# A two-layer bi-WKV and mixture-of-experts kernel: shared tiles at other steps, one exponential per unit of layer 1, and a fixed order in layer 1's input stage

## The chip, the cores and the metric

The kernel runs on one core of one Trainium2 chip, in fp32 throughout. The metric is the device time of one launch in microseconds (us), here the median of three runs. A core has five engines that run side by side, each through its own list of instructions in order: PE (TensorE: matmuls and transposes), DVE (VectorE), ACT (ScalarE: activations and copies), POOL (GpSimd: indirect gathers and scatters) and SP (SyncE, which here only issues transfers). They wait for each other through semaphores. ACT has to load a table (1.28 us in this trace) when it changes between families of functions, here between exponential and logarithm, sigmoid, and SiLU.

## The reference, cut to what matters

`x` is (4, 512, 512): 4 batches of 512 tokens with 512 channels, 2048 tokens in all. Two layers each add their result to `x`:

```python
def bi_wkv(r, k, v, w, u, time_emb):          # called with r = x, k = v = fside
    tf = sigmoid(sum(time_emb))               # one number per batch
    decay = exp(-exp(w)) * (0.5 + 0.5 * tf)   # per channel and batch
    ek = exp(min(k, 30)); ekv = ek * v
    nf, df = forward scans over tokens of ekv and ek:  a = a * decay + ekv_t
    nb, db = the same scans backward
    euk = exp(min(u + k, 30))
    num = nf + nb - ekv + euk * v
    den = df + db - ek + euk
    return sigmoid(r) * (num / max(den, 1e-8)) * (0.8 + 0.2 * tf)

x = x + ffn0(bi_wkv(x, fside, fside, w0, u0, cond))
x = x + ffn1(bi_wkv(x, fside, fside, w1, u1, cond))
```

`ffn0` normalises its rows (RMS norm with a weight), sends each token to the 2 best of 8 experts (`silu(h Wg) * (h Wu)` with 256 inner channels, then `Wd`), and adds a shared expert of the same form for all tokens. `ffn1` sends each token to the 6 best of 32 experts (352 inner channels, at most 512 tokens an expert) and adds a shared expert with 704 inner channels.

## The kernel before

**Tiles and units.** P is 128. The tokens are 16 tiles of 128 (NT); the channels are 4 blocks of 128 (NC). Layer 0's scans work on 16 units (b, c): one batch and one block of channels, 128 channels on the partitions by 512 tokens. `kA` holds k turned, `zT` the output of bi-WKV turned (channels on the partitions), `acc` rows of x or gathered rows. PSUM, the memory that matmuls write to, [...] given out by name: "tr" (turned tiles) 2, "den" 2, "num" 1, "g" 2, "pl" 1 in layer 0.

**Layer 0's steps.** The loop at L657 has a step for each unit and one more. Step n holds `sums(n-1)` (PE adds the forward and backward terms of num and den of the unit before), `front(n+1)`, `front_exps(n+1)` (two exponentials on ACT), `mid(n)` (the scans, on DVE), `back(n-1)` (the quotient: ACT makes `r`, the reciprocal, out of den with three activations at L448 to L450, DVE multiplies), `turn(n+3)` (k's transposes), and, at certain steps, the routing of a batch (`route_*`, `write_slots`, with POOL's writes of a table), `row_turn` and `row_out` (z turned back to rows for the gathers) and `logits0`. On the four compute engines the order is the order of the code (a manual schedule).

**Shared tiles of layer 0.** The shared expert runs tile by tile: `share_up` (PE, 16 matmuls at L594), `share_silu` (ACT), `share_hid` (DVE), `share_turn` (PE transposes at L612, ACT copy at L614), `share_down` (PE, four matmuls at L622), `share_put` (ACT copy, and SP writes the rows to `xb`). `pairs0` places tiles at steps: the up in the step that is its key, the hidden product one step later, turn, down and put two steps later. Tiles 0 to 5 are placed so; `early` is the first tile after them. Tiles 6 to 12 run in the tail after the loop (L722 to L764), with the down of a tile one turn of the loop behind its own transposes. Tiles 13 to 15 (from LATE) run after the routed experts (L979 to L990), where a down follows its own turn.

**Exponentials for layer 1.** Layer 1's scans need exp of k plus a bias twice per unit (`ek` and `euk`). `exps1_upto` (L643, L644) writes both into tiles that are free: 10 units by the end of the tail, and 6 units inside the routed stage, where `wkv1_rest` puts twelve exponentials and two table loads (L956 to L958) on ACT between the first and the second token tile of expert 1.

**Routed experts.** `routed` (L769) goes through experts and token tiles of 128 slots: POOL gathers rows, PE turns them (`pza`), ACT copies them out with a scale (`zgT`, L814), PE multiplies (`pgate` L862, `pup` L866), ACT and DVE make the hidden rows, PE turns them (`phT`), multiplies down (`pout`, L838), and POOL scatters and adds to `xa` or `xb`. DVE runs layer 1's scans (`wkv1`) beside it. In the text (1,2) is token tile 2 of expert 1.

**Layer 1's input stage (L993 to L1035).** For each token tile: DVE adds the summands (L1015, L1017), PE turns the result (`pt`, L1020), ACT takes the sigmoid (`sx`, L1022), DVE multiplies with `kA` into `zT` (L1023), PE makes 32 logits (`plg`, L1025) and turns `zT` back (`pz`, L1030), ACT copies the rows (`zr`, L1032), and SP writes them to `z1d`. Tiles 13 to 15 come first. Here the order on SP is fixed, and that of the other engines is left to the framework's scheduler. After it come layer 1's shared expert with its routing (L1107 to L1119) and its routed experts.

Of the kernel before, what the change touches and what calls it, by code (L numbers as in the profile page):

```python
# [18 lines left out]
P = 128  # L19
# [12 lines left out]
def adaln_ffn_kernel(  # L32
# [88 lines left out]
    banks.update(pool=ps, tr=2, den=2, num=1, g=2, pl=1)  # L121
# [97 lines left out]
    for l in range(2):  # L219
# [18 lines left out]
        decay.append((dec, cap, lom, inv))  # L238
    neg_min = const.tile([P, 1], F32, name="neg_min")
# [34 lines left out]
    def scans(l, b, c, v):  # L274
# [6 lines left out]
        nc.vector.tensor_scalar(v[:, :, 0], v[:, :, 0], inv, None, ALU.mult)  # L281
        for h in range(2):
            nc.vector.tensor_tensor_scan(v[:, h, :], dec.to_broadcast([P, S]), v[:, h, :], 0.0, ALU.mult, ALU.add)
# [146 lines left out]
    def mid(n):  # L430
# [6 lines left out]
        scans(0, b, c, v)  # L437
# [194 lines left out]
    rows, cols = [acc[:, t, :] for t in range(NT // 2)], [zcols(n) for n in range(NU)]  # L632
    spare = rows[:2] + cols[:4] + rows[2:] + cols[4:12]
    e1 = {}
    done = 0

    def exps1_upto(m):
        nonlocal done
        while done < m:
            b, c = units[done]  # L640
            kT = kA[:, c, b * S : (b + 1) * S]
            ek, euk = e1[done] = spare[2 * done], spare[2 * done + 1]
            nc.scalar.activation(ek, kT, AF.Exp, bias=decay[1][2][:, c, b : b + 1])  # L643
            nc.scalar.activation(euk, kT, AF.Exp, bias=uch[1][:, c : c + 1])  # L644
            done += 1


    pairs0 = {7: (0, 1), 10: (2, 3), 13: (4, 5)}
    early = 6
# [7 lines left out]
    for n in range(NU + 1):  # L657
# [36 lines left out]
        for t in pairs0.get(n, ()):  # L694
            share_silu(t)
        if c == 3 and b + 1 < NB or n == 0:
            sigmoids(b + 1 if n else 0)
        if n in pairs0 or c == 3 and b + 1 < NB or n == 0:
            nc.scalar.preload_act_table_set(EXP_LN)
        if n < NU:  # L700
            mid(n)
# [4 lines left out]
        if c == 2 and b >= 1:  # L706
            route_max(b - 1)
        if c == 3 and b >= 1:
            route_top(b - 1)
            route_pay(b - 1)  # L710
        if n == NU:
            share_up(early)
# [4 lines left out]
        if n >= 12:  # L717
            exps1_upto(n - 11)
# [3 lines left out]
    pz = [row_turn(t, "den" if t % 2 else "tr") for t in range(NT - TB, NT)]  # L722
    logits0(NB - 1)
    route_v(NB - 1)
# [5 lines left out]
    row_out(*pz[3])  # L730
    share_up(early + 1)
    share_silu(early)
    share_silu(early + 1)
# [14 lines left out]
    share_hid(early + 1)  # L748
    share_turn(early)
    for t in range(early + 2, LATE):  # L750
        share_up(t)
        share_silu(t)
        share_turn(t - 1)
        share_down(t - 2, "den")
        share_hid(t)
        share_put(t - 2)
        if t == 10:
            exps1_upto(8)
    share_turn(LATE - 1)
    for t in (LATE - 2, LATE - 1):  # L760
        share_down(t, "den")
        share_put(t)
    exps1_upto(10)
    nc.scalar.preload_act_table_set("silu_and_others")  # L764
    order.close()
# [165 lines left out]

    late_out = [zT[:, h, :S] for h in range(NT - LATE)]
    with tc.tile_pool(name="r0", bufs=1) as rp, tc.tile_pool(name="px0", bufs=1, space=PSUM) as px:
        third[0] = rp.tile([P, W0], F32, name="third0")
        for n in range(10, NU):
            spare += [rp.tile([P, S], F32, name=f"spare{n}_{h}") for h in range(2)]


        def wkv1(n):
            b, c = units[n]  # L940
            kT = kA[:, c, b * S : (b + 1) * S]
            ek, euk = e1[n]
            v = rp.tile([P, 2, S], F32, tag="v2", name=f"v2_{n}", bufs=1)
            cap = decay[1][1][:, c, b : b + 1]
            nc.vector.tensor_scalar(v[:, 0, :], ek, cap, None, ALU.min)
            nc.vector.tensor_tensor(v[:, 1, :], v[:, 0, :], kT, ALU.mult)
            scans(1, b, c, v)
            d, s = v[:, 0, :], v[:, 1, :]
            nc.vector.scalar_tensor_tensor(d, euk, E30, d, ALU.min, ALU.add)
            nc.vector.scalar_tensor_tensor(euk, euk, E30, kT, ALU.min, ALU.mult)  # L950
# [210 lines left out]
```

## Time and profile before

| | |
|---|---|
| time, three runs | 1561.48, 1562.08, 1569.90 us; median 1562.08 |
| the profiled execution | 1565.78 us; its span in the trace is 1563.8 us |
| busy over the span | PE 1424.2 us (91%), DVE 678.2 (43%), POOL 564.6 (36%), ACT 415.2 (27%) |
| instructions | 16280 |
| moved by transfers | 184.98 MB |

The profile comes from one execution. Every row of its timeline has a start, a length, the engine, the line of the code, the tiles written and read, and, in square brackets, how long the engine had been idle before and what ended that. The granted clock is the clock of PE as a share of full speed; it is either full or half at a moment, so that 0.78 over a stretch means that nearly half of it ran at half clock. PE's idle time is the time to look for wherever PE is the bound; in the first stage it is DVE's.

The stages by their times: layer 0's steps up to some 208 us, its tail to 258.8, the routed experts of layer 0 to 519, the three late shared tiles to 545, layer 1's input stage to 592.5, and the rest of layer 1 to the end.

### The profile page before, as it was taken

The numbers are of one execution on the slowest core, as the hardware profiler recorded it, in microseconds if no ns is written. First come the engines' busy times: TensorE is split into PE (matmuls) and PEld (weight loads), VectorE is DVE, ScalarE is ACT, GpSimd is POOL, SyncE is SP. The second block draws the span as 40 slices with busy tenths as digits, with TensorE's granted clock in tenths as the row PEclk, the third lists the DMA queues.
The fourth block names the chain that finished last, engine by engine and source line by source line (L and its number), as shares of the span: only waits on it lengthen the run. The fifth ranks groups of instructions, "written<-read, shape, count | busy, mean of one in ns | idle before, by whom it ended". The sixth has DMA issues, their size and how long they took to land. (4 is left out here: it accounts for less than half of the span.)

```text
span 1563.8 us, 16280 instructions
## 1 busy us (share of the span) xinstructions
PE 1424.2 (91%) x5033; PEld 849.2 (54%) x5033; DVE 678.2 (43%) x1189; ACT 415.2 (27%) x984; POOL 564.6 (36%) x563
## 2 busy tenths in 40 slices
PE   5778888989788788999999999999999999999997
PEld 3344456757566584444444555655655555555554
DVE  7999844999991145431111222222222222222221
ACT  6657626564344341000001111111111111111110
POOL 1020232756655100056662333344434343343332
PEclk9889889989998888999999999999999999999999
DMA  9301115544545560001115554656636485555442
GB/s 340 128 14 41 41 39 170 89 100 74 132 96 135 180 233 37 1 1 56 48 56 168 138 152 113 172 165 175 170 86 161 123 271 118 147 163 147 113 97 43
DMA packets 117932, 184.98 MB, mean 118 GB/s; under 512 B 19480, under 2 KB 64556, under 8 KB 117784
## 3 DMA queue, kind: packets, MB, share of 16 engines
q1 hardware_dynamic: 81912, 125.54, 23.5%
q0 software_dynamic: 35296, 56.63, 19.5%
q8 instruction: 67, 1.10, 0.3%
q10 hardware_dynamic: 576, 1.05, 0.2%
q14 instruction: 81, 0.66, 0.1%
HBM read 151.28 MB, written 52.64 MB: 130 GB/s over the span
## 5 line engine op out<-in xcount | busy, mean ns | idle before, releaser
L862 PE MATMUL pgate<-w,zgT 128*128 128x352 f32 (+1 forms) x656 | 198.3, 448 | 19.9 <-ACTq L920 9.3
L838 PE MATMUL pout<-w,hT 128*128 128x512 f32 (+1 forms) x432 | 201.2, 598 | 4.9 <-ACT hT L829 4.1
L866 PE MATMUL pup<-w,zgT 128*128 128x352 f32 (+1 forms) x656 | 192.1, 437 | 0.0
L843 POOL DMA_INDIRECT out_dram<-ob,put x52 | 82.9, 1595 | 281.6 <-DVE ob L842 147.7
L797 POOL DMA_INDIRECT acc<-z1d,put x119 | 123.2, 1035 | 134.6 <-PE pza L810 65.4
L862 PEld LDWEIGHTS pgate<-w,zgT 128*128 128x128 f32 x656 | 126.1, 200 | 76.1 <-issue 17.5
L365 POOL DMA_INDIRECT table<-pay,r1sloti x96 | 93.3, 972 | 191.3 <-DVE hid L1110 164.6
L878 DVE SCALAR_TENSOR_TENSOR hrow<-pup,tab,sgt 128x352 f32<-128x352 f32 x84 | 49.1, 584 | 255.1 <-issue 131.2
L866 PEld LDWEIGHTS pup<-w,zgT 128*128 128x128 f32 x656 | 125.5, 195 | 49.9
L842 DVE COPY ob<-pout 128x512 f32<-128x512 f32 x84 | 58.1, 692 | 174.4 <-PE pout L838 167.2
L838 PEld LDWEIGHTS pout<-w,hT 128*128 128x128 f32 (+1 forms) x432 | 76.8, 192 | 71.7 <-issue 54.1
L365 POOL DMA_INDIRECT table<-r0pay,r0sloti x32 | 34.1, 1064 | 184.6 <-DVE r0sloti L355 167.0
L833 ACT COPY hT<-phT 96x128 f32<-96x128 f32 x84 | 21.9, 261 | 287.0 <-DVE hT L831 287.0
L810 PEld LDWEIGHTS pza<-ident,acc 128*128 128x128 f32 x584 | 71.8, 141 | 44.9 <-issue 27.5
L820 ACT COPY zgT<-pza 128x256 f32<-128x256 f32 x103 | 38.3, 372 | 209.7 <-DVE zgT L819 158.0
L1107 PE MATMUL g<-zT,w 128*128 128x512 f32 (+1 forms) x192 | 88.1, 602 | 3.6 <-DVE lg L1039 3.6
L810 PE MATMUL pza<-ident,acc 128*128 128x128 f32 x584 | 86.5, 273 | 5.1 <-DMA acc<-z0d,put 2.5
L838 PE MATMUL pout<-zT,hT 128*128 128x512 f32 (+1 forms) x192 | 87.8, 593 | 0.0
L1107 PE MATMUL u<-zT,w 128*128 128x512 f32 (+1 forms) x192 | 86.3, 592 | 0.0
L1116 PE MATMUL o<-w,hid 128*128 128x512 f32 (+1 forms) x192 | 83.8, 592 | 0.0
L797 POOL DMA_INDIRECT acc<-z0d,put x51 | 62.5, 1225 | 58.5 <-issue 17.0
L862 PE MATMUL pgate<-zT,zgT 128*128 128x352 f32 x256 | 81.0, 459 | 0.0
(268 smaller groups left out, 2070.4 us busy)
## 6 DMA issues: line engine op xcount, KB each, us to landing
w<-in_L_ffn_w_dram SPq DMA_DIRECT2D x44, 704.0 KB, 4.6
zT<-in_L_ffn_w_dram SPq DMA_DIRECT2D x20, 704.0 KB, 5.9
w<-in_L_ffn_w_dram SPq DMA_DIRECT2D x22, 512.0 KB, 8.5
zT<-in_L_ffn_w_dram SPq DMA_DIRECT2D x10, 512.0 KB, 4.5
w<-in_L_ffn_w_dram SPq DMA_DIRECT2D x22, 192.0 KB, 8.5
acc<-in_x_dram SPq DMA_DIRECT2D x4, 1024.0 KB
xa<-acc SPq DMA_DIRECT2D x4, 1024.0 KB, 11.2
z0d<-zr SPq DMA_DIRECT2D x16, 256.0 KB, 2.0
```

Source lines behind the costliest of these rows:

```text
L365: ins = nc.gpsimd.indirect_dma_start(out=table, out_offset=bass.IndirectOffsetOnAxis(ap=sloti[:, t, j : j + 1], axis=0), in_=pay[:, t, j, ...
L797: nc.gpsimd.indirect_dma_start(out=rows(e, s), out_offset=None, in_=zd, in_offset=bass.IndirectOffsetOnAxis(ap=put_at[:, e * NS + s : e * ...
L810: nc.tensor.transpose(pza[which][:, c * P : (c + 1) * P], rows(e, s)[:, c * P : (c + 1) * P], ident)
L820: nc.scalar.copy(dst[:, h:, :], pza[which][:, h * P :].rearrange("p (c t) -> p c t", c=h))
L838: nc.tensor.matmul(po, hT[:m, j, :], dv[:m, j, :], start=(j == 0), stop=(j == nf - 1))
L842: nc.vector.tensor_copy(row, po)
L843: nc.gpsimd.indirect_dma_start(out=outs[n % len(outs)], out_offset=bass.IndirectOffsetOnAxis(ap=at, axis=0), in_=row, in_offset=None, boun ...
L862: nc.tensor.matmul(pg, zt[:, c, :], gv[:, c, :], start=(c == 0), stop=(c == NC - 1))
L866: nc.tensor.matmul(pu, zt[:, c, :], uv[:, c, :], start=(c == 0), stop=(c == NC - 1))
L878: nc.vector.scalar_tensor_tensor(hrow, pu, tab[:, col, 1:2], sgt, ALU.mult, ALU.mult)
L1107: nc.tensor.matmul(p[:m], wv[:, c, f : f + m], zT[:, c, cols], start=(c == 0), stop=(c == NC - 1))
L1116: nc.tensor.matmul(po, hid[:m, j, i * P : (i + 1) * P], dv[:m, j, :], start=(j == 0), stop=(j == len(FCH) - 1))
```

## The change

In layer 0 the shared tiles go to steps 6, 10, 14 and 15 (seven tiles instead of six), their SiLU comes after the step's other ACT work, and in the tail each down follows directly on its own turn. The PSUM banks go from two to one for "den" and from two to three for "g".

For layer 1 one exponential per unit is made instead of two. The second comes from it on DVE, by a factor per channel and batch (`ratio`, made once at the start). All sixteen are made in the steps from 8 on and in the tail, and `wkv1_rest` is gone. Two units of `wkv1` run in the tail, cut into steps by `yield`.

In layer 1's input stage the order on ACT, PE and DVE is written out: the turn of the next tile, then logits and rows of this one, then the product of the next. Tile 12 joins tiles 13 to 15 at the head, with loads of its own.

```diff
-    banks.update(pool=ps, tr=2, den=2, num=1, g=2, pl=1)
+    banks.update(pool=ps, tr=2, den=1, num=1, g=3, pl=1)
...
+    ratio = const.tile([P, NC, B], F32, name="ratio")
+    nc.vector.tensor_tensor(ratio, uch[1].unsqueeze(2).to_broadcast([P, NC, B]), decay[1][2], ALU.subtract)
+    nc.scalar.activation(ratio, ratio, AF.Exp)
...
-            ek, euk = e1[done] = spare[2 * done], spare[2 * done + 1]
-            nc.scalar.activation(ek, kT, AF.Exp, bias=decay[1][2][:, c, b : b + 1])
-            nc.scalar.activation(euk, kT, AF.Exp, bias=uch[1][:, c : c + 1])
+            nc.scalar.activation(e1[done], kA[:, c, b * S : (b + 1) * S], AF.Exp, bias=decay[1][2][:, c, b : b + 1])
             done += 1
...
+    def wkv1(n, pool, bufs):
+        b, c = units[n]
+        kT, e = kA[:, c, b * S : (b + 1) * S], e1[n]
+        v = pool.tile([P, 2, S], F32, tag="v2", name=f"v2b_{n}", bufs=bufs)
+        d, s = v[:, 0, :], v[:, 1, :]
+        nc.vector.tensor_scalar(d, e, decay[1][1][:, c, b : b + 1], None, ALU.min)
+        nc.vector.tensor_tensor(s, d, kT, ALU.mult)
+        nc.vector.tensor_scalar(e, e, ratio[:, c, b : b + 1], E30, ALU.mult, ALU.min)
+        yield
+        yield from scans(1, b, c, v)
...
-    pairs0 = {7: (0, 1), 10: (2, 3), 13: (4, 5)}
-    early = 6
+    pairs0 = {6: (0, 1), 10: (2, 3), 14: (4, 5), 15: (6,)}
+    early = 7
...
-        for t in pairs0.get(n, ()):
-            share_silu(t)
...
+        exps1_upto(max(0, n - 7) if n < 12 else min(2 * n - 18, 12))
+        for t in pairs0.get(n, ()):
+            share_silu(t)
+        if n in pairs0:
+            nc.scalar.preload_act_table_set(EXP_LN)
...
+    share_turn(early - 1)
     share_up(early + 1)
+    exps1_upto(NU)
     share_silu(early)
-    share_silu(early + 1)
+    share_down(early - 1, "den")
...
+    scans1 = (step for n in range(ahead1) for step in wkv1(n, wk, 3))
+    for t in range(early + 1, LATE):
+        if t > early + 1:
+            share_up(t)
         share_silu(t)
         share_turn(t - 1)
-        share_down(t - 2, "den")
+        share_down(t - 1, "den" if t % 2 else "num")
         share_hid(t)
-        share_put(t - 2)
-        if t == 10:
-            exps1_upto(8)
+        share_put(t - 1)
+        next(scans1, None)
+        next(scans1, None)
     share_turn(LATE - 1)
-    for t in (LATE - 2, LATE - 1):
-        share_down(t, "den")
-        share_put(t)
-    exps1_upto(10)
+    share_down(LATE - 1, "den")
     nc.scalar.preload_act_table_set("silu_and_others")
+    share_put(LATE - 1)
+    through(scans1)
...
-        def wkv1_rest():
-            exps1_upto(NU)
-            nc.scalar.preload_act_table_set("silu_and_others")
-            for n in range(10, NU):
-                wkv1(n)
...
-            for n in range(10):
-                wkv1(n)
+            for n in range(ahead1, NU):
+                through(wkv1(n, rp, 2))
...
-                {1: wkv1_rest, E0 - 2: shared_again, E0 - 1: lambda: scale_weights(*shared0[:2])},
+                {E0 - 2: shared_again, E0 - 1: lambda: scale_weights(*shared0[:2])},
...
+    first = [*range(LATE, NT), LATE - 1]
...
+    with tc.manual_schedule(
+        engines={mybir.EngineType.Activation, mybir.EngineType.PE, mybir.EngineType.DVE}
+    ):
+        turns = first + list(range(LATE - 1))
+        add(turns[0])
+        add(turns[1])
+        product(turns[0], gate(turns[0]))
+        for i, t in enumerate(turns):
+            if i + 2 < NT:
+                add(turns[i + 2])
+            if i + 1 < NT:
+                sx = gate(turns[i + 1])
+            rows_out(t)
+            if i + 1 < NT:
+                product(turns[i + 1], sx)
```

`gate(t)` is `pt` and the sigmoid `sx`, `product(t, sx)` the product into `zT`, and `rows_out(t)` is `plg`, `pz`, the copy `zr` and the write to `z1d`: the same operations as before, cut into functions.

## The prediction

> **What bounds the kernel now.** I read the rows of slices first, then the stages that the change touches, then single rows. Columns in the first fence are 40 slices of 39.1 us in tenths; in the second start:end, length, busy us (instructions) of PE, PEld, DVE, ACT, POOL, granted clock, DMA share, GB/s.
>
> ```profile
> PE   5778888989788788999999999999999999999997
> DVE  7999844999991145431111222222222222222221
> PEclk9889889989998888999999999999999999999999
> ```
> ```profile
> 0.00:258.80 258.80, 195.90 (x681) 112.56 (x682) 191.04 (x443) 151.28 (x277) 45.27 (x61) 0.92 0.30 106
> 258.80:519.00 260.20, 226.14 (x933) 165.35 (x934) 211.12 (x208) 123.20 (x366) 149.70 (x116) 0.93 0.49 109
> 519.00:545.00 26.00, 22.06 (x72) 14.40 (x71) 4.73 (x8) 4.38 (x11) 1.58 (x1) 0.90 0.61 190
> 545.00:592.50 47.50, 37.30 (x256) 34.38 (x256) 19.89 (x33) 19.81 (x34) 0.00 (x0) 0.78 0.68 241
> 592.50:1563.80 971.30, 942.80 (x3092) 522.53 (x3092) 251.44 (x501) 116.52 (x298) 368.07 (x385) 1.00 0.44 116
> ```
> These are layer 0's steps and tail, its routed experts, the three late shared tiles, layer 1's input stage, and the rest of layer 1. PE is the bound of the last 971 us, which no edit touches. In the first stage DVE is the bound until about 208:
> ```profile
> 100.00:120.00 20.00, 14.22 (x45) 6.32 (x46) 19.20 (x36) 10.49 (x25) 9.15 (x8) 0.91 0.09 29
> ...
> 208.80:258.80 50.00, 42.03 (x161) 27.96 (x161) 11.12 (x58) 27.09 (x52) 17.31 (x19) 0.96 0.33 109
> ```
> and PE in the tail. The lowest clock, 0.78, stands in the stage whose order is fixed by the change.
>
> **The change part by part.** All sums are against the profiled execution, 1565.78 us with a span of 1563.8; it stood 3.7 above the median, 1562.08, and I carry the difference over to the median.
>
> *One constant at the start.* `ratio` is a small DVE operation (neighbours there take 0.18) and a small Exp (0.20) between the ACT work of `lom` at 13.08 and the copy of `kA` at 13.20, with hand-overs: +0.6, between 0 (the first sums wait for k's load as well) and +0.7.
>
> *Shared tiles moved to other steps.* Steps run at 19.2 of 20 us on DVE, so PE work moved between them (3.5 us an up, 1.9 a down) is hidden by DVE and worth nothing either way. The one step where DVE waits is 14:
> ```profile
> 179.21 0.16 DVE L519 TENSOR_TENSOR v<-v,rsg 128x4 f32<-128x4 f32 x1 [4.71 <-ACT rsg L512]
> ```
> ACT came late because it stood behind the SiLU of tiles 4 and 5, whose sums PE ended at 173.6. With these two a step later and the SiLU behind the exponentials, 4.7 us of DVE go. But tiles 4 and 5's turn and down (3.7) and the up of tile 7 (3.5) then stand on PE ahead of the last row turns: row turns end near 207.8 instead of 208.85. So 1 of the 4.7 arrives.
>
> In the tail one up less remains (tiles 8 to 12 instead of 7 to 12), but `share_down` now follows its own turn, and waits for the copy between. The late tiles already run so:
> ```profile
> 538.48 1.98 PE L622 MATMUL pout<-third,shT 128*128 128x512 f32 x4 [0.61 <-ACT shT L614]
> ```
> They repeat each 6.26 us (531.23 to 537.49 at L612) where the tail has 5.39 (225.18 to 230.57). Four exponentials (0.62 each) and a table load (1.28) stand on ACT ahead of tile 7's SiLU, so I put the up of tile 9 near 223.8, where before that of tile 8 starts at 220.03. Four periods of 6.26 and a last turn and down of 2.7 end at 251.5; before, the last down ends at 252.5: −1 (−4 if the loop keeps 5.39, +3 if the exponentials reach PE in full).
>
> Two DVE units of layer 1 (13.2 us each) go into the tail beside 11 us of DVE work in 50: hidden by PE, ending near 253.
>
> *Exponentials and table loads between the tail and routed tile (0,0).* Two table loads and the exponentials that filled ACT from 253.18 to 258.33 go. That looks like −5. But the first `zgT` copy, at 258.34, also waits for the last shared row written by SP:
> ```profile
> 253.19 0.32 SPq L629 DMA_DIRECT2D xb<-so_rows  x1
> ...
> 258.40 0.37 SPq L142 DMA_DIRECT2D third<-in_L_ffn_w_gate_dram  x1
> ```
> SP's own next load of `third` waits for the same write and goes at 258.40, so that write took 5.1 us, in a queue with 512 KB of weights on either side. The order on SP is kept. So 0, as long as the write keeps its 5.1 us. The gathers and POOL's table writes have some 7 us to spare and stay covered.
>
> *Exponentials in routed tiles.* These are on the path. PE's first gates of (1,0) and (1,2), then the same of expert 2, which has no exponentials beside it:
> ```profile
> 326.20 1.97 PE L862 MATMUL pgate<-w,zgT 128*128 128x256 f32 x8 [1.25 <-PEq L920]
> ...
> 347.86 1.91 PE L862 MATMUL pgate<-w,zgT 128*128 128x256 f32 x4
> 386.31 1.53 PE L862 MATMUL pgate<-third,zgT 128*128 128x256 f32 x6 [2.15 <-PEq L920]
> ...
> 401.83 1.46 PE L862 MATMUL pgate<-third,zgT 128*128 128x256 f32 x6
> ```
> 21.66 against 15.52: 6.1, and 1.16 for the gate at 347.86, which runs at half clock after the stall (3.05 where a warm one takes 1.89): −7.1. ACT was blocked for 10 us (333.44 to 343.50), but expert 2 shows waits on its gather and on POOL that would appear in expert 1 too, so I don't take the 10. DVE's scans, now with one exponential multiplied up to two on DVE (still about 13.2 a unit), end after 14 units near 441 instead of 477, and are first needed at 545: 0.
>
> *Layer 1's input stage.* Per tile: four transposes (`pt`), a sigmoid, a product, eight small logit matmuls (`plg`), four transposes (`pz`). Before, a scheduler ran `pt` of several tiles ahead and left `pz` for the end; now each tile is `pt` of the next, `plg`, `pz`. At full clock a tile takes some 1.9 us (0.47 + 0.81 + 0.47 and hand-overs), at half clock 0.88 + 1.57 + 0.89 = 3.34. So all turns on the clock:
> ```profile
> 548.50:561.50 13.00, 13.00 (x63) 12.81 (x64) 4.74 (x8) 3.55 (x7) 0.00 (x0) 0.50 1.03 366
> 561.50:562.00 0.50, 0.50 (x5) 0.27 (x4) 0.20 (x1) 0.27 (x1) 0.00 (x0) 0.68 0.93 341
> 562.00:582.00 20.00, 18.87 (x166) 17.72 (x166) 12.02 (x19) 9.97 (x19) 0.00 (x0) 1.00 0.34 118
> ```
> PE's records are unbroken from 548.5 to 561.5 and the clock stayed at 0.50. All clock changes of this trace lie on a grid of 3.413 us, so I worked out for each grid window how much of it streamed columns (128 columns at half clock: 0.213 us). Of windows at half clock, the 19 that went up had at least 0.797, the 13 that stayed at most 0.735; of windows at full clock, the 19 that dropped had at most 0.345 and the lowest that stayed had 0.391. The four here had 0.609, 0.588, 0.505 and 0.797; the last held twelve transposes in a row.
>
> [...] by the rows its share is (512 + 256 + 512 columns = 2.134 us) / 3.34 = 0.64, under 0.735, and it never comes up again. [...]
>
> Does it fall at all? After `pt` of the first two tiles (ended at 546.55 on the old time line) PE now waits for the table load (546.40, 1.28), sigmoid (0.60) and product (0.69), to 549.2: 2.65 us of 3.413 empty, against a wait of 1.66 at 548.34 before, which was enough to fall. It holds only if the grid cuts the gap in halves with work on both sides.
>
> Cold: 549.2 + 16 × (1.57 + 0.89) + 14 × 0.88 = 600.9; the clock falls only at the end of the gap's window, so some work after the gap still runs at full clock (−0.9); from the end of the last `pz` (588.96) to the first matmul of the shared stage (592.56) stand 3.6 more. 603.6 against 592.56: +11 (+7 if windows with runs of `pz` and `pt` back to back bring the clock up half-way, +13 if hand-overs show as gaps). Warm: 549.2 + 16 × 1.9 + 3.6 = 583.2: −9.4. The loads, 8.4 MB from 534 at 366 to 390 GB/s, are in by 556 and bound neither, so tile 12's own pair of loads and the earlier pool cost nothing; `z1d` writes are now 3.3 us apart, so that three `zr` buffers suffice.
>
> Sum: +0.6 − 1 + 0 − 7.1 + 11 = +3.5: 1569.3 against the profiled 1565.78, or 1565.6 against the median.
>
> **The rivals.** *The input stage stays warm.* For it: windows with a share of 0.391 stayed at full clock, and a warm mix streams about half of its time (1.07 of 1.9 us), so once warm it stays warm. Against it: the gap of 2.65 us at its head. It gives 3.5 − 11 − 9.4 = −16.9: 1545.2.
>
> *Slower: one bank for `den`.* Sums of unit n now can't start before the ACT reads of unit n−1's `den` are over. Between these DVE has about 9.1 us of cover (the rest of `back` 2.1, `front` 0.9, `mid` 6.1) for 1.8 to 3.4 of sums, 2.05 of Relu, Ln and Exp, and queueing on both engines. If queueing passes 4, each late step costs the rest; 1.5 us at 10 of 16 steps is +15: 1581. Against it: PE is busy 14 of 20 us there, so queues are short.
>
> *The exponentials' gain isn't there:* expert 1 keeps 21.66 because the gather or POOL is late instead. That is +7.1: 1572.7.
>
> **How the numbers follow.** The forecast has 0.65, warm 0.20, the bank 0.08, no gain 0.07. The forecast's own bounds are the start (0 to 0.7), the tail (−4 to +3), the routed gain (−10 to −5) and the cold stage (+7 to +13): 1557 to 1573. About 0.5% (7.8 us) is what a measurement of this kernel can tell from no change. Of the 0.65, 0.50 lies within it and 0.15 above; warm is faster (0.20); the bank and most of the lost gain (0.05) are slower, the rest within: slower 0.28, same 0.52. The range leaves out most of the bank: 1543 to 1576.
>
> **What would show it.** Right: DVE's wait of 4.71 at step 14 gone; the first `zgT` copy still about 5 us behind the last shared row's issue; expert 1's first to third gate near 15.5; in the input stage a granted clock near 0.5 over some 50 us, with `pt` rows at 0.88 a tile. Wrong: that stage at clock 1.0 within 36 us; or DVE waits on `r` at each step.

## The result and the profile after

The changed kernel takes 1576.03 us (median of six runs, 1574.61 to 1578.09), the kernel before beside it 1566.47 us (six runs, 1561.48 to 1572.99): a ratio of 1.0062, 95% interval 1.0035 to 1.0089. It is slower by 0.6%, 9.6 us, where +3.5 us (0.2%) was forecast, and just above the upper end of the range, 1576. Part of the distance to the forecast time of 1565.6 is its base: the 1562.08 of the first three runs was low, the median of six is 4.4 us higher, and in the three later comparisons before's median was 1569.53, 1572.09 and 1569.87. The profiled execution has a span of 1572.8 us against 1563.8.

The page's slices of the changed kernel (columns as before):

```profile
PE   4878877989788799999999999999999999999997
DVE  7999858999950235431111222222222222222221
PEclk9899999999998958999999999999999999999999
```
In the row of the clock the fifteenth slice, 550 to 590 us, is 5 where before it was 8: layer 1's input stage, 541 to 598. The same stages as before, cut at the same instructions:

```profile
0.00:262.60 262.60, 194.84 (x681) 112.13 (x681) 215.46 (x472) 148.57 (x275) 46.87 (x61) 0.92 0.30 104
262.60:514.80 252.20, 220.06 (x932) 160.96 (x932) 187.70 (x196) 112.85 (x350) 147.57 (x116) 0.95 0.50 110
514.80:541.00 26.20, 21.07 (x73) 13.83 (x73) 4.04 (x7) 5.95 (x14) 1.58 (x1) 0.93 0.68 211
541.00:598.10 57.10, 51.27 (x256) 50.46 (x256) 20.81 (x34) 20.00 (x33) 0.00 (x0) 0.54 0.56 201
598.10:1572.80 974.70, 945.71 (x3092) 524.13 (x3092) 251.57 (x500) 116.61 (x298) 368.16 (x385) 0.99 0.44 116
```
The input stage is 57.1 us instead of 47.5, at a clock of 0.54 instead of 0.78, with PE busy for 51 of 57. Cut more finely, by the starts of matmuls on PE, one profile against one profile:

| from, to | before | after | change | forecast |
|---|---|---|---|---|
| start, last logits of layer 0 (`pl`) | 208.81 | 208.54 | −0.27 | } −0.4 together |
| to the last down of the tail (last `so` matmul) | 43.09 | 47.40 | +4.31 | } |
| to the first gate of the routed experts | 6.91 | 6.72 | −0.19 | 0 |
| routed experts and late tiles, to the first `pt` | 286.78 | 278.32 | −8.46 | −7.1 |
| input stage, to the shared stage's first matmul | 46.97 | 57.14 | +10.17 | +11 |
| to the last matmul | 961.33 | 964.99 | +3.66 | 0 |

The terms for the transition, the routed experts and the input stage hold within 1.4 us here. Two don't: the tail, and the part behind the edit. The other profiles on record show how firm each row is. The start took 205.3 to 208.8 us in six profiles with before's steps (the one in the table is the slowest; mean 206.6), and 207.8 to 209.8 in twelve with the changed ones (mean 208.9), so that the steps lost some 2.3 us rather than won 0.3. The tail took 41.9 to 43.1 us in before's order and 46.8 to 49.1 in seven profiles with the changed one. The routed experts took 286.1 to 288.6 us in five profiles with before's exponentials and 272.6 to 284.3 (mean 277.9) in eleven with the changed ones. The lines of the changed kernel are numbered some 20 higher behind the edit: L862 is L885, L838 is L861, L622 is L626.

**Steps and tail.** Windows of a step and of the tail:

```profile
100.00:120.00 20.00, 18.11 (x63) 8.39 (x62) 19.34 (x34) 13.20 (x27) 9.39 (x8) 0.94 0.15 53
208.50:262.60 54.10, 40.19 (x146) 24.83 (x144) 35.44 (x85) 19.06 (x43) 14.73 (x15) 0.91 0.30 99
```
DVE still bounds the steps, though PE has four more busy microseconds in this one. Its wait of 4.71 at step 14 is gone; the waits over 1 us that it has in the steps are 1.85 at 73.25 and 2.59 at 197.12, where PE's `pos` is late (before had a wait of 3.84 on it too, at 202.52, which the prediction passed over). After the steps it waits longer than before: 8.87 us at 211.57 for ACT's squares, where before has 3.30 at 210.49. The end of the steps came near the time put down (the row turns end at 208.6 us; 207.8 was forecast, and 0.6 for the constant), but the gain against before is luck: before's profile was its slowest of six up to there, and on the average nothing is left of the 4.7 us of DVE.

In the tail before shows turn and down back to back, each 5.39 us after the last:

```profile
225.18 0.38 PE L612 MATMUL sph<-ident,shr 128*128 128x128 f32 x2
225.40 1.88 PE L622 MATMUL so<-w,shT 128*128 128x512 f32 x4
...
230.57 0.38 PE L612 MATMUL sph<-ident,shr 128*128 128x128 f32 x2
```
In the changed kernel PE shows:

```profile
224.47 3.75 PE L626 MATMUL so<-w,shT 128*128 128x512 f32 x4 [3.04 <-DVE counts L765]
228.02 3.94 PE L598 MATMUL sg<-w,zT 128*128 128x256 f32 x16
231.80 0.38 PE L616 MATMUL sph<-ident,shr 128*128 128x128 f32 x2
232.78 1.98 PE L626 MATMUL so<-w,shT 128*128 128x512 f32 x4 [0.61 <-ACT ssg L603]
```
The period of 6.26 us with its wait of 0.61 is there as forecast, but it starts at 228.02 instead of 223.8. The first row says why: tile 7's down waits 3.04 us for DVE's copy of the expert counts (`counts`), which reads the "num" bank that this down wants. The down then runs at half clock, 3.75 us for 1.98. The clock had fallen before that wait: the window that ends at 221.84 streams 0.19 of its time, as PE has only small matmuls there and waits 1.54 us for tile 7's hidden row. The second profile of the changed kernel has the same wait, 3.02 us.

**Between the tail and the first gate:**

```profile
257.23 0.32 SPq L633 DMA_DIRECT2D xb<-so_rows  x1
...
262.23 0.37 SPq L142 DMA_DIRECT2D third<-in_L_ffn_w_gate_dram  x1
```
```profile
262.07 1.14 ACT L837 ACTIVATE zgT<-pza,chan 128x128 f32<-128x128 f32 x4 [4.87 <-DMA xb<-so_rows]
```
ACT is free now, and `zgT` still comes 4.84 us after the last shared row is issued (5.15 before). Nothing was gained by removing the exponentials there.

**The routed experts:** first and third gate of expert 1, the same of expert 2.

```profile
328.37 1.99 PE L885 MATMUL pgate<-w,zgT 128*128 128x256 f32 x8 [0.81 <-ACTq L943]
...
346.38 2.76 PE L885 MATMUL pgate<-w,zgT 128*128 128x256 f32 x8
...
383.21 1.99 PE L885 MATMUL pgate<-third,zgT 128*128 128x256 f32 x8 [0.81 <-ACTq L943]
```
18.01 us from the first to the second row, where 21.66 was before and 15.5 forecast. The rest of the gain lies on either side: to expert 2's first gate it is 6.95 us from the routed stage's start (127.50 to 120.55), for a forecast of 7.1. The whole stage is 8.46 us shorter in this pair of profiles and about 9 on the average of those on record, with a spread of 12 us in the changed order.

**The input stage:**

```profile
544.38 1.08 PE L1031 MATMUL plg<-gateT,zT 128*128 128x32 f32 x8 [2.30 <-DVE zT L1025]
...
549.78 1.75 PE L1031 MATMUL plg<-gateT,zT 128*128 128x32 f32 x8
551.34 1.09 PE L1036 MATMUL pz<-ident,zT 128*128 128x128 f32 x4
552.23 1.06 PE L1018 MATMUL pt<-ident,acc 128*128 128x128 f32 x4
...
598.12 6.67 PE L1129 MATMUL g<-zT,w 128*128 128x512 f32 x8 [3.55 <-DVE lg L1061]
```
The gap at the head (2.30 us; forecast 2.65), then the regular turn of `plg`, `pz`, `pt`, 3.31 us a tile (forecast 3.34), without a gap in PE's records. Thirteen grid windows in a row stream 0.625 to 0.656 of their time (forecast 0.64), and all thirteen stay at half clock. The last row is the head of the shared stage: its first eight matmuls need 6.67 us instead of before's 5.37. PE's clock is at half there up to 604.13, for 6.01 us of them; in before it is so up to 595.95, for 3.39 us.

**The rest of layer 1.** Of the +3.66 us behind the edit, 1.3 are this head. Two waits before `phT` matmuls grow by some 0.4 us each. The rest is one window at half clock (1266.32 to 1269.73), far behind the edit, at a gate of one of layer 1's experts:

```profile
1266.97 3.90 PE L885 MATMUL pgate<-w,zgT 128*128 128x352 f32 x8
```
Before's row at the same place ran at full clock:

```profile
1259.04 2.53 PE L862 MATMUL pgate<-w,zgT 128*128 128x352 f32 x8
```
In the changed kernel PE had waited 2.24 us just before it, in before 1.83. The second profile of the changed kernel has a wait of 2.17 us at this place and no half clock behind it.

### The profile page after: what moved, and what is told of

It is laid out like the page before. It is cut to its first block, busy times and chain, and to the rows that moved or that the text cites. A ratio compares the mean times of both kernels' runs of the same rounds, so it can differ in the third digit from the quotient of the medians.

```text
span 1572.8 us, 16267 instructions
## 1 busy us (share of the span) xinstructions
PE 1433.0 (91%) x5033; PEld 861.5 (55%) x5033; DVE 679.6 (43%) x1206; ACT 404.0 (26%) x967; POOL 564.2 (36%) x563
## 5 line engine op out<-in xcount | busy, mean ns | idle before, releaser
L885 PE MATMUL pgate<-w,zgT 128*128 128x352 f32 (+1 forms) x656 | 197.5, 446 | 17.8 <-PEq L943 7.0
L861 PE MATMUL pout<-w,hT 128*128 128x512 f32 (+1 forms) x432 | 200.1, 595 | 1.4 <-DVE hT L854 0.8
L885 PEld LDWEIGHTS pgate<-w,zgT 128*128 128x128 f32 x656 | 125.2, 198 | 73.9 <-issue 26.0
L901 DVE SCALAR_TENSOR_TENSOR hrow<-pup,tab,sgt 128x352 f32<-128x352 f32 x84 | 49.1, 584 | 255.9 <-issue 131.2
L861 PEld LDWEIGHTS pout<-w,hT 128*128 128x128 f32 (+1 forms) x432 | 76.4, 191 | 67.4 <-issue 53.5
L861 PE MATMUL pout<-zT,hT 128*128 128x512 f32 (+1 forms) x192 | 87.8, 593 | 0.0
L842 DVE COPY zgT<-pza 128x256 f32<-128x256 f32 x103 | 43.0, 418 | 88.6 <-PE pup L889 87.8
```

The lines of the kernel that those rows point to most:

```text
L842: nc.vector.tensor_copy(dst[:, :h, :], pza[which][:, : h * P].rearrange("p (c t) -> p c t", c=h))
L861: nc.tensor.matmul(po, hT[:m, j, :], dv[:m, j, :], start=(j == 0), stop=(j == nf - 1))
L885: nc.tensor.matmul(pg, zt[:, c, :], gv[:, c, :], start=(c == 0), stop=(c == NC - 1))
L901: nc.vector.scalar_tensor_tensor(hrow, pu, tab[:, col, 1:2], sgt, ALU.mult, ALU.mult)
```

## The experiments

Each ratio is to the kernel before on the same chip. Where one stage is the question, its length from the trace is the measure, since times of one kernel spread over 10 to 20 us here.

**The order of the input stage.** First the stage is given back to the scheduler, with the loads at its head kept.

```diff
-    with tc.manual_schedule(
-        engines={mybir.EngineType.Activation, mybir.EngineType.PE, mybir.EngineType.DVE}
-    ):
-        turns = first + list(range(LATE - 1))
...
+    for t in first + list(range(LATE - 1)):
+        add(t)
+        product(t, gate(t))
+        rows_out(t)
```


> The changed kernel with layer 1's input stage left to the scheduler again (the loads at its head kept). Theory (the fixed order costs its +10.2 us because it never streams 0.75 of a 3.413 us window, so that PE's clock stays at half to 600.7): the stage, from the first pt to the first matmul of the shared stage, takes some 47 us instead of 57.1, its clock comes back to 1.0 within about 15 us, and the time is 10 us under the changed kernel's, near 1566. Rival (the fixed order is no worse, the stage is slow because of what comes before it: the tile 12 load, the earlier pool, the earlier start): the stage keeps 57 us and the time stays at 1576.

It missed: 1573.34 us, ratio 1.0023 (1.0002 to 1.0043), and the stage took 56.8 us, from 538.14 to 594.95.

```profile
538.10:594.90 56.80, 48.95 (x256) 46.49 (x256) 19.32 (x32) 19.58 (x33) 0.00 (x0) 0.61 0.57 197
```
The clock was at half for 44.5 of these. This scheduler's order isn't that of before (tile 12 is at the head, loads and start are elsewhere): its one run of eleven transposes, 552.46 to 555.1, is cut by the grid at 553.9, and the two windows have 0.720 and 0.656. So the run doesn't undo the edit, and it doesn't refute the rival, whose 57 us it shows. The opposite experiment is the kernel before with only the new input stage, its order and its loads (L993 to L1035 replaced):

> The kernel before with only the fixed order of layer 1's input stage and its loads. Theory: the stage goes from 47.0 to about 57 us at a granted clock of 0.5, and the head of the shared stage loses up to 1.3 more: 10 to 13 us slower than before, 1577 to 1579. Rival as above: no change, 1566.

1577.58 us, ratio 1.0049 (1.0033 to 1.0065).

```profile
541.50:600.00 58.50, 52.64 (x256) 52.00 (x256) 20.75 (x34) 20.10 (x33) 0.00 (x0) 0.53 0.56 199
```
The stage is 58.6 us against 47.0: the fixed order with its loads costs 11.6 us there, with nothing else changed. The medians are 8.05 us apart. Neither run parts the order from the load of tile 12. The trace of the changed kernel does: in the thirteen cold windows PE waits for no load, and the next runs shorten the stage with the same loads.

**Is it the clock?** The gap at the head is filled with work that nobody reads.

```diff
-    banks.update(pool=ps, tr=2, g=2, o=1)
+    banks.update(pool=ps, tr=2, g=2, o=1, x=1)
...
+    def fill(t, n):
+        px = bank("x", f"fill{t}")
+        for i in range(n):
+            c = i % NC
+            nc.tensor.transpose(px[:, c * P : (c + 1) * P], acc[:, t, c * P : (c + 1) * P], ident)
...
+            if i == 0:
+                fill(t, 20)
             rows_out(t)
```


> The changed kernel with 20 more transposes (into a PSUM bank that nobody reads, output unchanged) where PE waits 2.30 us for the first product of layer 1's input stage. They take 0.11 us each at full clock, 2.2 us, so they fill the gap and nothing else. Theory: the clock doesn't fall at the head of the stage, a tile takes 2.0 us instead of 3.3, and the stage 38 to 40 us instead of 57.1: 16 to 20 us under the changed kernel, 1556 to 1560, and faster than before. Rival (the clock falls in this stage whatever PE does at its head, or falls again because a warm tile streams only half of its time): 57 us again, plus up to 2: 1576 to 1578.

1572.89 us, ratio 1.0023 (1.0006 to 1.0041); the stage 56.2 us. Neither theory holds for the whole stage: it falls into three parts.

```profile
538.60:550.90 12.30, 12.18 (x108) 11.67 (x108) 7.07 (x11) 5.63 (x9) 0.00 (x0) 1.00 1.05 389
550.90:556.10 5.20, 0.16 (x2) 0.00 (x0) 0.68 (x2) 1.80 (x4) 0.00 (x0) 0.80 0.95 359
556.10:594.70 38.60, 35.04 (x168) 34.64 (x168) 12.94 (x23) 12.09 (x21) 0.00 (x0) 0.50 0.36 124
```
```profile
554.30 0.59 ACT L1038 COPY zr<-pz 128x512 f32<-128x512 f32 x1 [6.00 <-DMA z1d<-zr]
```
The clock stays at 1.0 for the first tiles, 1.7 to 1.9 us each. Then ACT waits 6.00 us for one of three `zr` buffers, whose write to `z1d` hasn't landed: it was issued behind loads that run at 389 GB/s. PE waits 5.10 us, the clock goes from 1.00 to 0.50, and the rest takes 3.31 us a tile. Beside the fill, the next run has eight buffers:

```diff
+    zq = zst.enter_context(tc.tile_pool(name="z2", bufs=2))
...
-        zr = zp.tile([P, D], F32, tag="zr", name=f"zr1_{t}", bufs=3)
+        zr = zq.tile([P, D], F32, tag="zr", name=f"zr1_{t}", bufs=8)
```


> The kernel with 20 filling transposes at the head of the input stage, and eight zr buffers instead of three, from memory that the routed stage has left. Theory (with the gap filled the clock stays up, and then ACT's copy waits for a zr buffer, 6.00 us, because the z1d writes stand behind the loads; that wait is the second gap in which the clock falls): no wait of PE over 1 us in the stage, clock 1.0 throughout, 1.75 us a tile, the stage 3.4 + 28 + 4.7 = 36 to 38 us instead of 56 to 57, and about 18 us under the changed kernel: 1556 to 1558. Rival (PE waits for the loads of the next tiles themselves, not for the buffers): the wait of 5 us moves to an add, the clock falls again near 551, the stage keeps 52 to 56 us and the time 1573.

1546.98 us, ratio 0.9857 (0.9818 to 0.9896).

```profile
550.00:581.70 31.70, 30.72 (x276) 29.81 (x276) 21.34 (x35) 18.73 (x33) 0.00 (x0) 1.00 0.77 284
```
31.7 us instead of 57.1, with 276 matmuls instead of 256. That is shorter than the 36 to 38 us put down, and the time lower than the 1556 to 1558: a tile takes 1.72 us. The same order that lost 10 us at half clock wins 15 at full clock.

The last of this group leaves the gap and three buffers as they are, and puts the extra work into the middle of the cold stage (`if i == 4: fill(turns[0], 32)`).

> The changed kernel with one burst of 32 more transposes before the logits of the fifth tile of layer 1's input stage, its gap at the head left as it is (output unchanged). Theory (at half clock it is the share of streamed columns in a 3.413 us window that counts; PE's records leave no gap there already): the burst streams 0.95 of a window, the clock comes up inside it, and the eleven tiles after it take 1.75 to 2.0 us instead of 3.31: 15 to 17 us won for 5 to 6 of burst, the stage about 46 us, the time 10 us under the changed kernel, 1566. Rival (the clock is held at half in this stage by something else, as the 14 windows without a gap in PE's records suggest): it stays at half, and the burst costs its 6.8 us: 1583.

1560.92 us, ratio 0.9942 (0.9925 to 0.9960).

```profile
543.20:556.50 13.30, 13.30 (x64) 13.30 (x65) 6.30 (x10) 4.09 (x7) 0.00 (x0) 0.50 1.05 369
556.50:561.80 5.30, 5.30 (x34) 5.30 (x33) 1.29 (x2) 0.64 (x2) 0.00 (x0) 0.65 0.38 142
561.80:582.50 20.70, 20.48 (x186) 19.81 (x184) 11.74 (x18) 11.43 (x21) 0.00 (x0) 1.00 0.61 202
```
PE is busy without a gap in the first two and for 20.48 of 20.70 us in the third, and the clock is 0.50, then comes up in the burst, then is 1.00. What differs in PE's records is how densely columns stream: 0.59 to 0.66 of the grid windows in the first row, 1.00 of the one that brought the clock up. The stage is 46.3 us, 10.8 less than in the changed kernel with the 5.3 us of work for nothing paid.

**The tail.** The banks of the downs are exchanged, so that tile 7's goes to "den".

```diff
-        share_down(t - 1, "den" if t % 2 else "num")
+        share_down(t - 1, "num" if t % 2 else "den")
...
-    share_down(LATE - 1, "den")
+    share_down(LATE - 1, "num")
```


> The changed kernel with the two PSUM banks of the tail's downs exchanged, so that tile 7's down no longer goes into the bank that holds the counts until DVE has copied them. Theory (the +4 us at the end of layer 0's tail is this wait of 3.04 us with the half clock behind it): PE goes from tile 7's turn to its down without that wait, the up of tile 9 starts near 224 instead of 228.0, the first gate of the routed experts near 258.6 instead of 262.66, and the time is 4 us lower: 1572. Rival (tile 8's SiLU and hidden row, behind route_slots on DVE, hold the tail anyway): the wait moves to tile 8's turn, and the first gate stays within 1 us of 262.66.

1572.60 us, ratio 1.0032 (1.0014 to 1.0050). The wait on the counts is gone, and tile 9's up starts 2.7 us earlier, at 225.35:

```profile
222.55 3.01 PE L626 MATMUL so<-w,shT 128*128 128x512 f32 x4 [0.46 <-ACT shT L618]
```
From the last `pl` to the last down it takes 45.33 instead of 47.40: half of the forecast's 4 (the time of 1572.60 meets its 1572 all the same, by luck). The down and the up after it still run partly at half clock (3.01 and 4.33 us), because the window with the wait for the hidden row, 1.52 us here, streams 0.27 and the clock falls at its end, 223.38; and a later down waits 1.20 us for ACT once. An attempt to keep the clock up there, with 14 transposes into the "pl" bank behind the counts' matmul and the banks exchanged, was spoilt by its own wait:

> The changed kernel with the exchanged banks of the tail and, beside it, 14 more transposes into a free bank where PE waits 1.5 us for tile 7's hidden row (output unchanged). With the exchanged banks alone tile 7's down and the up of tile 9 still ran partly at half clock (3.01 us for a down that takes 1.98, 4.33 for an up that takes 3.62), and the first gate came only 1.4 us earlier. Theory (the rest of the tail's +4 us is the clock that falls in the waits of PE around 214 to 222): the down takes 1.98 and the up 3.62, and from the last logits (pl) to the last down of the tail 44 us instead of 45.3 with the banks alone and 47.4 in the changed kernel. Rival (the rest is ACT's and DVE's order, the exponentials ahead of the SiLU): no change against the banks alone.

```profile
223.88 3.18 PE L764 MATMUL fill<-ident,acc 128*128 128x128 f32 x14 [3.76 <-DVE r0addr L349]
```
The positions of the slots lie in that bank until DVE has read them. The tail took 48.17 us, the kernel 1577.80 us, ratio 1.0050 (1.0032 to 1.0068). PE stood still where the gap was to be filled, the 14 transposes ran at half clock (0.213 us each, 2.98 us to the next matmul), and the run doesn't tell how much a warm tail would win. The other way, each down one turn behind again (only the loop is shown; the downs before and after the loop move too, and the last goes into "num"):

```diff
-        share_down(t - 1, "den" if t % 2 else "num")
+        share_down(t - 2, "den")
...
-        share_put(t - 1)
+        share_put(t - 2)
```


> The changed kernel with the tail's downs one turn of the loop behind their transposes again, as before the change (one den bank; the last down in num). Theory (a down right behind its own turn waits 0.61 us for the copy, so that the period is 6.26 us instead of 5.39, and the first one waits for the counts' bank): the period goes back to 5.4, PE doesn't wait for the counts, and from the last logits (pl) to the last down 41 to 42 us instead of 47.4: 5 to 6 us off the tail. DVE's second unit, which is paced by the hidden rows, then ends after PE and keeps 1 to 2 us of it. Rival (with one den bank each down waits for the put of the one before): the period stays above 6.

```profile
229.22 0.38 PE L616 MATMUL sph<-ident,shr 128*128 128x128 f32 x2
229.44 1.88 PE L626 MATMUL so<-w,shT 128*128 128x512 f32 x4
```
In the loop there is no wait between turn and down, a period of 5.39 us, 41.54 us from `pl` to the last down, 1567.84 us, ratio 0.9991 (0.9966 to 1.0016). One "den" bank suffices for this. It takes off all of the tail's loss (43.09 before) and 1.5 us more: the wait for the counts' bank, and the 0.87 us that each period of the changed tail is longer, which the forecast had.

**The transition.** Only the last shared row goes elsewhere.

```diff
-        so = wk.tile([P, D], F32, tag="so", name=f"so_rows{t}")
+        so = zT[:, 3, 2 * S : 3 * S] if t == LATE - 1 else wk.tile([P, D], F32, tag="so", name=f"so_rows{t}")
```


> The changed kernel with the last shared row of the tail copied into an unused part of zT instead of a tile whose memory the routed stage takes over. Theory (the first zgT copy waits 4.9 us for that row's write to land, only because the memory is reused): zgT starts within 0.6 us of the transposes' end and DVE's last scan product, near 258.3 instead of 262.07, and the first gate at 258.8 if its weights are there. Rival (the row of the profile names the load of w_up as what ended PE's wait: the weights, issued at 256.57 and 257.60, are what is late): the first gate stays at 262 to 263.

```profile
259.10 1.14 ACT L837 ACTIVATE zgT<-pza,chan 128x128 f32<-128x128 f32 x4 [1.16 <-DVE kA L665]
```
The first gate follows the last down after 2.84 us instead of 6.72. So the wait was for that row's write, and for its memory only; on PE's row the profile had named the load of `w_up`. What ends it now is DVE's second unit of layer 1. 1569.59 us, ratio 0.9994 (0.9976 to 1.0011).

**The exponentials in the routed tiles.** In the kernel before, `exps1_upto(NU)` and the table load in `wkv1_rest` are taken out; the six units of layer 1's scans that they fed use the tiles of other units.

> The kernel before without the twelve exponentials and two table loads in the routed tiles (six units of layer 1's scans then work on the tiles of other units). Theory (the prediction's step): from expert 1's first gate to its third 21.66 becomes 15.5 to 18, with gains on either side, and the first gate of expert 2 comes 7 us earlier; 7 us under before. Rival (ACT's whole block of 10 us is on the path): 10 us. Other rival (gathers on POOL take over at once): under 4.

```profile
323.21 1.97 PE L862 MATMUL pgate<-w,zgT 128*128 128x256 f32 x8 [1.73 <-PEq L920]
...
339.47 1.89 PE L862 MATMUL pgate<-w,zgT 128*128 128x256 f32 x8
...
376.30 1.97 PE L862 MATMUL pgate<-third,zgT 128*128 128x256 f32 x8 [1.69 <-PEq L920]
```
Only this stage is read, since layer 1 then routes other values: 16.26 us from expert 1's first to third gate (21.66), and 120.67 from the routed stage's start to expert 2's first gate (127.50): −6.8. It is the −7 of the forecast, not the 10 that ACT was blocked.

**Is the kernel before always at 47?** Three more profiles of it, and one of the changed kernel.

> The kernel before once more, unchanged, for a second profile. Theory (with the scheduler's order it depends on where the free-running grid of 3.413 us falls whether a window of layer 1's input stage streams enough to bring the clock up, and the first profile, 47.0 us, was one of the good cases): of this and the next two profiles at least one has the stage at 52 us or more, with the clock at half for over 25 us, and the time of each follows the stage. Rival (the order of before always comes up, and the spread of its times, 1557 to 1577 us, has other causes): 46 to 48 us in all three.

> As the run before it: the same kernel, a third profile. Theory: the stage is 47 or about 57 us, by the phase. Rival: 46 to 48 us.

> As the two runs before it: the same kernel, a fourth profile. Theory: the stage is 47 or about 57 us, by the phase. Rival: 46 to 48 us.

> The changed kernel once more, unchanged, for a second profile. Theory (its order streams 0.64 of every window, whatever the phase): the stage is 57 us at half clock again; the tail from the last logits (pl) to the last down 47 to 49 us, with the wait for the counts' bank. Rival (the first profile was an unlucky phase): the stage comes out near 47 us or less.

The stage took 48.1, 46.8 and 49.8 us in the kernel before, at half clock for 24, 20 and 27 us; its time was 1566.59, 1563.42 and 1565.20 us. None of the four profiles has the theory's 52 us or more. For the other runs this settles nothing: the four profiled executions took at most 1566.6 us, at a mean clock of 0.961 to 0.964, and 99 of the 136 runs of before beside the experiments took longer, up to 1577.8 us at 0.954. The times also spread widely where the scheduler orders the stage (1557 to 1578 in before, 1561 to 1580 with the scheduler's order in the changed kernel), and narrowly with the fixed order in the kernel before (1575 to 1583). That the stage stays cold in some runs of before is possible, and not shown.

The third of these profiles shows once more that busy is not enough. In the window from 564.83 PE is busy throughout, with 24 of the small logit matmuls in a row, and 0.336 of the window streams; the clock falls at its end:

```profile
564.83:568.24 3.41, 3.41 (x34) 3.41 (x33) 2.23 (x5) 1.19 (x2) 0.00 (x0) 1.00 0.00 0
568.25:571.65 3.40, 3.40 (x18) 3.03 (x18) 2.48 (x5) 1.35 (x3) 0.00 (x0) 0.50 0.02 5
```
The changed kernel took 57.0 us in the stage, with the wait of 2.30 us at its head once more, and 46.8 us in the tail. In all seven profiles with the fixed order, no fill and no burst the stage took 57.0 to 58.6 us, against 46.8 to 49.8 in before's four: the loss goes with the order. The time of the changed kernel, though, was 1566.81 us here, 7.8 less than that of the first profile: 4.5 of these lie in the routed experts and 3.2 behind the edit. So the sign of the whole change rests on the two medians of six, and single runs of the two kernels overlap. The window at half clock behind the edit came in some runs with the cold stage (964.9 to 965.1 us from the shared stage to the last matmul with the fixed order alone, the exchanged banks and the last row in `zT`) and not in others (961.5 to 962.5 with the scheduler's order, the late downs and the spoilt fill, after waits of up to 2.60 us at that place).

**All that helped, together.** Fill, eight buffers, exchanged banks and the last row in `zT`; and then the late downs instead of the banks, with one unit of layer 1's scans in the tail instead of two.

> The changed kernel with the filled gap, eight zr buffers, the exchanged banks of the tail, and the last shared row in zT (the three edits that each shortened their stage). Theory (they lie in different stages and add): 25 us for the input stage, 2 for the banks, 3 for the row, against the changed kernel's 1576: 1546. Rival (what one stage wins the next gives back, as the clock falls at other places): 1550 to 1555.

> As the one with all edits, but with the downs one turn behind as in the run on them instead of the exchanged banks, and with one unit of layer 1's scans in the tail instead of two, so that DVE is not the last there. Theory: 3 us more than with the banks, 1543. Rival: the unit that moves to the routed stage delays the gathers or hidden rows there, 1546 as with all edits.

1536.29 us, ratio 0.9783 (0.9735 to 0.9831), and 1530.39 us, ratio 0.9759 (0.9711 to 0.9808).

```profile
526.20:557.90 31.70, 30.72 (x277) 29.81 (x277) 21.38 (x35) 18.75 (x33) 0.00 (x0) 1.00 0.79 295
```
The stage has the same 31.7 us, from `pl` to the last down it is 41.56, and from there to the first gate 2.70. So each stage keeps its gain beside the others. Both times are lower than put down (1546 and 1543), by 10 and 13 us, and what makes this difference was not followed. The last version is 2.4% faster than the kernel before (1.9 to 2.9, from four runs).

## Why the prediction was wrong, and where it was right

The mechanism of the largest term and the sign of the sum were right, the size was not: the forecast lay at +3.5, the medians at +9.6, the two profiles at +9.2.

- The step that failed is the tail, "−1": it was +4.3. The sum had the order of instructions and the period of 6.26 right, and left out who else holds a PSUM bank. "num" holds the counts until DVE's copy, which stands behind `route_slots`; the first of the alternating downs asks for it, and waits 3.04 us. Tile 9's up came 4.2 us later than put down. With the banks exchanged the wait is gone and the up comes 2.7 us earlier; what remains is half clock, which begins with the wait of 1.5 us for tile 7's hidden row: the sum had put the exponentials ahead of that row, but not the clock that falls behind them. How much of the tail a warm clock would win stays open. The wait for the bank could be read ahead of time from the two texts: every name passed to `bank` and the last reader of its tile before.
- The steps are part of the same "−1". They ended near the time put down, but the base was a slow one: against the mean of before's profiles they lost some 2.3 us. The agreement of −0.27 with the forecast is luck.
- The input stage, the largest term, held in every number: the gap (2.30 for 2.65), the share (0.625 to 0.656 for 0.64), the turn (3.31 for 3.34), +10.2 for +11. Put into the kernel before by itself it cost 11.6. A sum by PE's busy time would have missed it: thirteen windows of 3.413 us in which PE was busy throughout stayed at half clock.
- The routed experts were right in sum (−8.5 here, −7 by the exponentials alone) and wrong in place: expert 1 keeps 18.0 instead of 15.5, and the rest is won around it, as the whole chain of gathers moves. The forecast's own parts, 6.1 and 1.16, make 7.3 and not 7.1. With a spread of 12 us over the profiles, agreement within 1.4 is partly luck.
- The transition was right: nothing from ACT's removed work, because a write was as late. That it waits for memory, not for data, came out only in the run with the row in `zT`; it was worth 3.9 us.
- "0" for the rest of layer 1 was +3.7 in the profile: 1.3 by the shared stage's head, 1.7 by the one window at half clock, and the rest by two waits. The second profile shows +0.5. It should have had a bound of its own in the range.
- The rival in which the stage stays warm was priced at 1.9 us a tile with "three buffers suffice". At 1.72 us a tile they don't, and it would have fallen back, as the run with the fill alone did.
- The rival of the one "den" bank did not come. PE did wait for that bank, 28.0 us in eight waits up to 212 us, but in steps that DVE paces; DVE waited for `r` once, for 0.4 us.

## What to carry to other kernels

Count what streams, not what is busy: if small matmuls follow each other in a fixed mix, work out the share of columns in it at half clock. At 0.625 to 0.656 PE stayed at half here for thirteen windows, and work for nothing gave back more than its price: with a burst of 5.3 us in it the stage was 10.8 us shorter. When a stage becomes faster, look for the next buffer that must hold what its transfers can't yet take: at 1.72 us a tile three `zr` buffers cost ACT a wait of 6.00 us. And for each use of a bank or a reused tile in a new place, write down its last reader, on which engine, and what is queued ahead of it.

## What the runs showed of the hardware

In the profiles of the kernel before and of the changed one PE's clock is 1.0 or 0.5 and nothing between, and its changes (39 and 29 of them) lie multiples of 3.413 us apart, within 0.003 us. This grid doesn't start with the program: counted from the span's start its edges lie 2.03 us behind a multiple of 3.413 in the first of the two profiles and 3.39 us in the second.

Streaming is counted as in the prediction: 128 columns are 0.213 us at half clock, and half of that at full clock. From the start of one such matmul to the next start the two profiles have medians of 0.213 and 0.109 us. In the changed kernel's profile 14 windows at half clock brought the clock up, with a share of 0.796 or more, and 26 didn't, with 0.741 at most; at full clock the 15 windows that lost it streamed at most 0.380, and the lowest that kept it 0.370. Over the eighteen profiles of these kernels there are 294 windows at half clock that streamed 0.70 or more: 273 brought the clock up, and 21 didn't (the highest of these 0.776). Of the 295 that streamed less, one did (0.664). At full clock all 274 windows that lost it streamed at most 0.39, and none that kept it streamed under 0.357. The groups overlap, so these are counts of this case and no limit.

The state then held. Once at half clock, the changed kernel's stage, with PE busy for 51 of its 57 us, had a mean of 0.54. Once at full clock, the same mix in the run with the fill and eight buffers, streaming 0.61 to 0.62 of its time at 1.72 us a tile, stayed at 1.00 for the 31.7 us of the stage.

In the run with the fill alone a `z1d` write issued at 544.18 behind loads running at 389 GB/s held its buffer until 554.3, where before's writes of this kind have a median of 2.2 us from issue to landing.
